# One block's gate projection as three float32r passes, and two sets of weight splits placed elsewhere

## The chip, the cores and the metric

The kernel runs on one core of one Trainium2 chip. The core has TensorE (PE: matmuls; PEld is its weight load), VectorE (DVE), ScalarE (ACT), GpSimd (POOL), SyncE (SP, which here issues the transfers) and DMA engines. The metric is the device time of the whole program in microseconds (us), less being better.

## The reference

The input x has 4 sequences of 1024 tokens with 512 features. Two sublayers follow one another, each as x + LN(f(LN(x))), where LN subtracts the mean and divides by the standard deviation.

- Retention: q = x Wq', v = x Wv', g = silu(x Wg'), all 512 wide. A scan over the tokens keeps state = lam * state + v for each feature, with lam set by `beta`; y = q * state is normalised over the features, scaled by gamma, shifted by beta, multiplied by g and projected by Wo.
- FFN: gate = silu((x Wgate) * scale), up = (x Wup) * scale, both 1536 wide; the product is projected back to 512 by Wdown. These three weights are rounded to 8-bit floats first.

## The kernel before

**Blocks.** The 4096 tokens are worked on as 8 blocks of 512 tokens (`NB` = 8, `TB` = 512), features on the partitions in 4 chunks of 128. A `Retention` object works one block through the first sublayer, an `Ffn` object one block through the second in 12 steps i = 0 to 11 (`gate`, `up`, `fuse`, `rest`, `down`). While the FFN of block t runs, the retention of block t+1 is woven into its steps. Blocks 0 and 1 come ahead of that loop: a straight list of calls (the "opening" in what follows) normalises and projects block 0 (object `a`) and projects block 1 (object `b`), and prepares weights.

**Order.** Every compute engine's instructions are kept in the order in which the Python code issues them (`InOrder`, which is line 75 in the profile, so that nearly every row there reads L75). An instruction that has to wait holds up all that follows on its engine. Waits come from data and from buffers.

**Two kinds of matmul.** In float32 one matmul instruction of 128x512 does it. In float32r the operands have fewer bits, so an exact product takes three passes over split operands: `top` (the upper bits), `low` (the rest, scaled), `diff`. `begin(k, c, home)` runs the passes top and low of column c of projection k into a PSUM bank and then has ACT multiply the bank by 1 + 2^-12 (the "rescale"); `end(k, c)` runs the pass diff on top of that and then uses the bank: for v two half scans and a copy of the carry on DVE, for q a product on DVE and a sum on POOL, for g a silu on ACT. Block 0 uses float32 for v, q, g and o (`v`, `q`, `gate`, `o`); block 1 uses passes for v, q and g, with weights in SBUF; blocks 2 to 7 use passes throughout, with weights that a ring of transfers brings (`w_ring`).

**Banks.** PSUM banks are named by `home`: `pa0` and `pa1`, two banks that share the name `pf` and are given out in turn, and `pd0` to `pd3`. In the opening the `pf` banks go to v and g of block 0, then to block 1; later the FFN's `gate` and `up` use them.

**Splits.** `Splitter.split(n)` prepares one 128-column unit of a weight: DVE cuts the upper bits, subtracts, and forms `diff`; ACT then scales `low`. Units 0 to 3 are of v, 4 to 7 of q, 8 to 11 of g, 12 to 15 of o. `store(n)` sends the parts to DRAM for the later blocks. In SBUF they lie in five slots taken in turn. The table `times` places the splits of o into block 1's FFN steps (keys are the FFN's block, step and place in it).

**FFN weights.** `rounds(n)` advances a generator that rounds FFN weights piece by piece: one DVE cast to 8 bits, one ACT copy into `gate_sb`, `up_sb` or `down_sb`, and an empty turn, with the load of a next piece in between.

**Block 0's norm of y.** `mean` averages y over the features by a matmul (`mu`), `center_y` subtracts it on DVE, squares on ACT and sums on POOL (`sqsum`; the squares have two buffers); `var`, `rstd_y` and `z` finish it, and `o` projects.

## Time and profile before

| | |
|---|---|
| median of 3 runs | 897.91 us (895.42 to 899.96) |
| the profiled execution | 896.99 us, of which 895.2 us is the span from first to last instruction |
| mean granted TensorE clock | 0.997 of full |
| PE busy | 879.5 us, 98% of the span |
| DVE busy | 627.0 us, 70% |
| ACT busy | 419.0 us, 47% |
| POOL busy | 234.1 us, 26% |

"Busy" is the time in which an engine has an instruction under way; idle time of an engine that is not the bottleneck costs nothing. Durations of matmuls overlap one another, so the spacing of their starts, not the duration of one, is what a stream of them costs.

### The profile page before, as it was taken

Reading aid. Unit: us, or ns where it says so; the run is one execution under the profiler, and the core shown is the slowest. Engines: PE = TensorE matmul, PEld = TensorE weight load, DVE = VectorE, ACT = ScalarE, POOL = GpSimd, SP = SyncE. Lnnn points to the kernel's source line nnn. Section 1 sums busy time; section 2 is a strip of 40 time slices with the busy share of each in tenths; the row PEclk is TensorE's granted clock in tenths of the full one; section 3 lists DMA queues with packets and bytes.
Section 4 is the critical chain, followed back from the end, with each engine's and each line's share of the span. In section 5 each row is a group of like instructions: output and inputs, shape, how many; then the busy total and the mean of one; then the engine's idle time right before and its main releaser. Section 6 shows DMA issues by size and latency. Waiting matters only on the chain.

```text
span 895.2 us, 11996 instructions
## 1 busy us (share of the span) xinstructions
PE 879.5 (98%) x3948; PEld 739.1 (83%) x3948; DVE 627.0 (70%) x1074; ACT 419.0 (47%) x741; POOL 234.1 (26%) x301
## 2 busy tenths in 40 slices
PE   9999999999999999999999999999999999999996
PEld 7466786788888888888888888888888888888885
DVE  4898796686777666876678675876758756665635
ACT  1369566433645336453454435453364533644323
POOL 1215203302414033230513214150232403322020
PEclk9999999999999999999999999999999999999998
DMA  8975544687464674556662765627745464424021
GB/s 283 288 240 180 179 148 147 170 249 251 131 169 149 204 235 146 137 172 214 220 173 71 250 205 178 188 72 247 236 140 153 143 210 141 140 96 118 1 95 50
DMA packets 115576, 152.67 MB, mean 171 GB/s; under 512 B 10867, under 2 KB 54644, under 8 KB 115444
## 3 DMA queue, kind: packets, MB, share of 16 engines
q1 hardware_dynamic: 114644, 151.18, 55.4%
q8 instruction: 33, 0.54, 0.2%
q10 hardware_dynamic: 864, 0.66, 0.2%
q14 instruction: 35, 0.29, 0.1%
HBM read 117.46 MB, written 38.54 MB: 174 GB/s over the span
## 4 chain that ended last, share of the span: by engine, by line
PE 84%; DVE 2%; ACT 1%; issue 0%; DVEq 0%
PE pfu L75 18%; PE pfg L75 18%; PE pd L75 17%; PE po L75 8%; PE pv L75 7%; PE pq L75 7%; PE pg L75 7%; PE mu L75 1%; PE pt L75 1%; PE var L75 0%; DVE gate L75 0%; DVE y L75 0%; DVE d L75 0%; DVE split_room L75 0%; DVE x1nT L75 0%
## 5 line engine op out<-in xcount | busy, mean ns | idle before, releaser
L75 PE MATMUL pfu<-x1nT,up_sb 128*128 128x512 f32 x768 | 183.1, 381 | 0.0
L75 PE MATMUL pfg<-x1nT,gate_sb 128*128 128x512 f32 x768 | 182.5, 380 | 0.1
L75 PE MATMUL pd<-down_sb,fuse 128*128 128x512 f32 x720 | 170.5, 379 | 0.0
L75 PEld LDWEIGHTS pfu<-x1nT,up_sb 128*128 128x128 f32 x768 | 145.1, 189 | 22.5 <-issue 1.7
L75 PEld LDWEIGHTS pfg<-x1nT,gate_sb 128*128 128x128 f32 x768 | 144.4, 189 | 22.6 <-ACT gate L75 1.9
L75 PEld LDWEIGHTS pd<-down_sb,fuse 128*128 128x128 f32 x720 | 141.4, 196 | 14.5
L75 DVE SCALAR_TENSOR_TENSOR gate<-pfu,us_sb,gate 128x512 f32<-128x512 f32 x96 | 71.7, 747 | 68.9 <-PE pfu L75 57.8
L75 ACT CAST fuse<-gate 128x512 fp32r<-128x512 f32 x90 | 55.6, 618 | 126.4 <-DVE gate L75 125.4
L75 ACT ACTIVATE gate<-pfg,gs_sb 128x512 f32<-128x512 f32 x96 | 65.7, 684 | 98.0 <-PE pfg L75 98.0
L75 POOL TENSOR_SCALAR mv<-mv 128x1 f32<-128x1 f32 (+1 forms) x82 | 22.1, 270 | 322.7 <-DVE mv L75 320.6
L75 DVE TENSOR_TENSOR fuse<-gate,fuse 128x512 fp32r<-128x512 f32 x90 | 69.9, 777 | 6.6 <-ACT fuse L75 6.4
L75 POOL TENSOR_TENSOR d<-d,x 128x512 f32<-128x512 f32 x28 | 42.1, 1524 | 84.5 <-ACT d L75 70.6
L75 DVE BATCH_NORM_STATS2 st<-x 128x6 f32<-128x512 f32 x64 | 43.5, 680 | 17.9 <-POOL x L75 15.1
L75 POOL TENSOR_TENSOR mv<-mv,nhalf 128x1 f32<-128x1 f32 (+1 forms) x75 | 52.1, 694 | 6.2
L75 POOL TENSOR_TENSOR x<-x,x1n 128x512 f32<-128x512 f32 x32 | 44.4, 1394 | 21.6 <-ACT x1n L75 17.4
L75 ACT ACTIVATE pv<-pv 128x512 f32<-128x512 f32 x28 | 16.3, 582 | 47.8 <-PE pv L75 47.8
L75 POOL TENSOR_TENSOR ysum<-y 128x512 f32<-128x512 f32 x8 | 10.6, 1324 | 106.7 <-DVE y L75 106.7
L75 DVE TENSOR_TENSOR y<-pq,y 128x512 f32<-128x512 f32 x28 | 19.1, 681 | 21.5 <-PE pq L75 21.5
L75 DVE BATCH_NORM_STATS2 st<-po 128x6 f32<-128x512 f32 x32 | 21.9, 684 | 14.3 <-PE po L75 14.3
L75 ACT ACT_TABLE_LOAD x19 | 24.4, 1283 | 15.0 <-DVE var L75 10.8
L75 POOL TENSOR_TENSOR sqsum<-sqsum,sq 128x512 f32<-128x512 f32 x21 | 29.2, 1389 | 7.2 <-PE pg L75 5.5
L75 DVE SCALAR_TENSOR_TENSOR y<-y,lnb_sb,mids 128x512 f32<-128x512 f32 x28 | 26.0, 928 | 7.1 <-ACT mids L75 7.0
(216 smaller groups left out, 1482.5 us busy)
## 6 DMA issues: line engine op xcount, KB each, us to landing
x<-in_x SPq DMA_DIRECT2D x52, 256.0 KB, 5.3
kept<-x SPq DMA_DIRECT2D x32, 256.0 KB, 3.2
x<-kept SPq DMA_DIRECT2D x32, 256.0 KB, 4.2
out<-d SPq DMA_DIRECT2D x31, 256.0 KB, 2.0
w_ring<-dtop_v SPq DMA_DIRECT2D x24, 256.0 KB, 4.3
w_ring<-dlow_v SPq DMA_DIRECT2D x24, 256.0 KB, 3.1
w_ring<-ddiff_v SPq DMA_DIRECT2D x24, 256.0 KB, 3.9
w_ring<-dtop_q SPq DMA_DIRECT2D x24, 256.0 KB, 2.6
```

The source lines that it names most:

```text
L75: return lambda *args, **kwargs: tc.keep_in_program_order(op(*args, **kwargs))
```

## The change

- **Block 0's g** is no longer four float32 projections but `begin` and `end` as in block 1. New code, `new_parts` and `parts_of_x`, makes the parts of block 0's normalised x early in the opening: for each quarter three DVE instructions and one ACT copy, into the parts of `gate_sb`, `up_sb` and `down_sb` that hold no FFN weights yet. The order becomes begin 0; mean and centring; begin 1, end 0; begin 2, end 1; begin 3, end 2, end 3. `gate`, `silu` and `g_of` go.
- **`end` is cut in two**, `close` (the diff pass) and `finish` (what uses the bank), and in block 1's v and q the DVE work is placed anew: `split(5)`, `split(6)` and `split(7)` come ahead of scans that they followed, and one FFN weight cast comes earlier.
- **`split` of o is cut in two**, DVE's three instructions and ACT's scaling (`lower`, letter l in `times`). In step 5 of block 1's FFN the DVE parts of units 14 and 15 both come at its start, ahead of `fuse`; the ACT parts come later.

The core of the diff:

```diff
-            act.activation(low, m, AF.Copy, scale=1.0 / LOW)
             self.at_work[n] = {"diff": diff} if k == "o" else {"diff": diff, "low": low}
+            self.lows[n] = low
+            if k != "o":
+                self.lower(n)
+        def lower(self, n):
+            low = self.lows.pop(n)
+            act.activation(low, low.bitcast(F32), AF.Copy, scale=1.0 / LOW)
...
-            (0, 11, "mid"): "w12 w13 w14 w15", (1, 0, "start"): "r s12", (1, 0, "mid"): "s13",
-            (1, 0, "end"): "k12", (1, 1, "start"): "k13", (1, 5, "start"): "s14",
-            (1, 5, "mid"): "k14 s15", (1, 5, "end"): "k15",
+            (0, 11, "mid"): "w12 w13 w14 w15", (1, 0, "start"): "r s12", (1, 0, "mid"): "l12 s13",
+            (1, 0, "end"): "k12", (1, 1, "start"): "l13 k13", (1, 5, "start"): "s14 s15",
+            (1, 5, "mid"): "l14 k14", (1, 5, "end"): "l15 k15",
...
+        def new_parts(self):
+            self.tops, self.low = (w[:, :, 2 * P : 2 * P + TB] for w in (gate_sb, up_sb))
+            self.diff = down_sb[:, 2 : 2 + NC, :]
+        def parts_of_x(self, k):
+            top = work.tile([P, D], F32, tag="tok", name=f"top_{self.t}_{k}", bufs=4)
+            top = top.rearrange("p (c g j) -> p c g j", c=NC, j=Q)
+            x, low, diff = self.quarter(self.xnT, k), self.quarter(self.low, k), self.quarter(self.diff, k)
+            dve.tensor_scalar(top.bitcast(I32), x.bitcast(I32), TOP_MASK, None, ALU.bitwise_and)
+            act.copy(self.quarter(self.tops, k), top)
+            dve.tensor_tensor(low, x, top, ALU.subtract)
+            dve.scalar_tensor_tensor(diff, low.bitcast(F32), -1.0 / LOW, top, ALU.mult, ALU.add)
...
+    a.new_parts()
+    for k in range(2):
+        a.parts_of_x(k)
     decay()
+    for k in range(2, NS):
+        a.parts_of_x(k)
...
-    a.g_of(0, "pf")
+    a.begin("g", 0, "pf")
     a.mean()
     a.center_y()
     splitter.store(11)
-    a.g_of(1, "pf")
+    a.begin("g", 1, "pf")
+    a.end("g", 0)
     b.cut_x(2)
     b.cut_x(3)
     rounds(3)
-    a.g_of(2, "pf")
+    a.begin("g", 2, "pf")
+    a.end("g", 1)
     splitter.split(0)
-    a.gate(3, "pf")
-    a.silu(3)
+    a.begin("g", 3, "pf")
+    a.end("g", 2)
+    a.end("g", 3)
     a.var()
...
     a.o_moments(3)
+    rounds(1)
     a.x1_moments(2)
     a.x1_of(3)
-    b.end("v", 0)
+    b.close("v", 0)
     b.begin("v", 2, "pd0")
+    b.finish("v", 0)
     a.x1n_of(2)
     a.rest_of(0)
-    b.end("v", 1)
+    b.close("v", 1)
     a.turn_x1n(1)
     a.upper_of(1)
+    b.begin("v", 3, "pd1")
+    splitter.split(5)
+    splitter.store(4)
     a.x1_moments(3)
-    b.begin("v", 3, "pd1")
     a.x1n_of(3)
     a.rest_of(1)
-    splitter.split(5)
-    splitter.store(4)
-    b.end("v", 2)
+    b.close("v", 2)
     a.turn_x1n(2)
     a.upper_of(2)
     b.begin("q", 0, "pd2")
-    a.rest_of(2)
-    b.end("v", 3)
-    b.begin("q", 1, "pd3")
     splitter.split(6)
     splitter.store(5)
+    b.finish("v", 1)
+    a.rest_of(2)
+    b.close("v", 3)
+    b.begin("q", 1, "pd3")
     a.turn_x1n(3)
     a.upper_of(3)
-    b.end("q", 0)
+    b.close("q", 0)
     splitter.split(7)
     splitter.store(6)
+    b.finish("v", 2)
+    b.finish("q", 0)
+    b.begin("q", 2, "pf")
+    b.close("q", 1)
     a.rest_of(3)
-    b.begin("q", 2, "pf")
-    b.end("q", 1)
-    rounds(1)
+    b.finish("v", 3)
+    b.finish("q", 1)
     b.begin("q", 3, "pf")
     b.end("q", 2)
-    rounds(2)
     b.end("q", 3)
     splitter.store(7)
-    rounds(3)
+    rounds(5)
```

More of the change, by code (lines that the diff above doesn't have):

```diff
@@ L330, in __init__ @@
             self.raw = {}
-            self.slots, self.slot_of, self.at_work = [], {}, {}
+            self.slots, self.slot_of, self.at_work, self.lows = [], {}, {}, {}
         def by_chunk(self, ap):
@@ L403, in sandwich @@
             (0, 1, "end"): "c12", (0, 2, "end"): "c13", (0, 3, "end"): "c14", (0, 4, "end"): "c15",
[3 rows of a table removed]
[3 rows of a table added]
         }
         def at(self, *when):
-            do = {"c": self.copy, "s": self.split, "k": self.store, "w": self.keep}
+            do = {"c": self.copy, "s": self.split, "l": self.lower, "k": self.store, "w": self.keep}
             for what in self.times.get(when, "").split():
@@ L607, in pass_of @@
                 w = splitter.part(k, c, part)
-            x = {"top": self.by_chunk, "low": self.low, "diff": self.diff}[part]
+            x = {"top": self.by_chunk if self.passes else self.tops, "low": self.low, "diff": self.diff}[part]
             for i in range(NC):
@@ L626, in end, with close, finish @@
         def end(self, k, c):
-            bank = self.bank.pop((k, c))
-            self.pass_of(bank, k, c, "diff")
-            bank = in_order(bank)
+            self.close(k, c)
+            self.finish(k, c)
+        def close(self, k, c):
+            self.pass_of(self.bank[k, c], k, c, "diff")
+        def finish(self, k, c):
+            bank = in_order(self.bank.pop((k, c)))
             if k == "v":
@@ L651, in end @@
                     pool.tensor_tensor(self.sum, self.sum, y[:, c, :], ALU.add)
-            else:
-                act.activation(self.new_mids()[:, c], bank, AF.Silu)
+            elif self.passes:
+                act.activation(self.new_mids()[:, c], bank, AF.Silu)
+            else:
+                home = big if c == 3 else work
+                tag, bufs = ("fuse", 3) if home is big else ("sg", 3)
+                self.g[c] = home.tile([P, TB], F32, tag=tag, name=f"g_{self.t}_{c}", bufs=bufs)
+                act.activation(self.g[c].rearrange("p (k u) -> p k u", k=2), bank, AF.Silu)
         def gap(self, n):
@@ L814, in rstd_y @@
             )
-        def gate(self, c, home="pa"):
-            self.pg[c] = ps_tile(f"pg_{self.t}_{c}", home)
-            project(self.pg[c], wg_sb, c, [self.by_chunk])
-        def silu(self, c):
-            home = big if c == 3 else work
-            tag, bufs = ("fuse", 3) if home is big else ("sg", 3)
-            self.g[c] = home.tile([P, TB], F32, tag=tag, name=f"g_{self.t}_{c}", bufs=bufs)
-            act.activation(self.g[c], self.pg.pop(c), AF.Silu)
-        def g_of(self, c, home="pa"):
-            self.gate(c, home)
-            self.silu(c)
         def scale_y(self, c):
```

## The prediction

> **What bounds the kernel now.** I read the page's busy shares and its chain first, then TensorE's waits, then the timelines around the three edits.

> ```profile
> PE 879.5 (98%) x3948; PEld 739.1 (83%) x3948; DVE 627.0 (70%) x1074; ACT 419.0 (47%) x741; POOL 234.1 (26%) x301
> PE 84%; DVE 2%; ACT 1%; issue 0%; DVEq 0%
> ```

> TensorE is the bound; only fewer PE cycles or fewer PE waits can save time. The waits view of PE lists all it ever waited for; its two largest entries are the targets of the second and third edit.

> ```profile
> PE pg L75 <- ACT pg L75: 2.4, 1, 2.4
> PE pq L75 <- ACT slot L75: 2.1, 1, 2.1
> ```

> The timeline of PE where the first edit falls (start, length of the group, count):

> ```profile
> 36.72 3.60 PE L75 MATMUL pq<-xnT,wq_sb 128*128 128x512 f32 x8
> 40.16 3.60 PE L75 MATMUL pg<-xnT,wg_units 128*128 128x512 f32 x8
> 43.59 1.02 PE L75 MATMUL mu<-ysum,mean_r 128*128 128x512 f32 x2
> 44.45 10.46 PE L75 MATMUL pg<-xnT,wg_units 128*128 128x512 f32 x24
> 54.75 1.02 PE L75 MATMUL var<-sqsum,mean_r 128*128 128x512 f32 x2
> ```

> No bracket with an idle time stands here: PE runs through. ACT in the same stretch:

> ```profile
> 43.81 0.63 ACT L75 ACTIVATE gate_sb<-gate_sb 128x512 fp32r<-128x512 f32 x1 [4.06 <-DVE gate_sb L75]
> 44.41 0.62 ACT L75 CAST down_sb<-top 128x512 fp32r<-128x512 f32 x1
> 45.05 1.28 ACT L75 ACT_TABLE_LOAD   x1
> 46.34 0.60 ACT L75 ACTIVATE g<-pg 128x512 f32<-128x512 f32 x1
> 46.84 0.62 ACT L75 ACTIVATE sqsum<-y 128x512 f32<-128x512 f32 x1
> 47.35 1.14 ACT L75 ACTIVATE sq<-y 128x512 f32<-128x512 f32 x2
> 49.36 0.63 ACT L75 ACTIVATE sq<-y 128x512 f32<-128x512 f32 x1 [0.87 <-POOL sqsum L75]
> ```

> The last square waits for POOL's first sum. The silu of g 0 stands ahead of the squares here; after the change it stands behind them.

> **Part 1, block 0's g.** Removed: four columns of 3.43 us (40.16 to 43.59), 13.7. Added: 48 float32r matmuls; the chain's rows have 8 in 1.73 us, 0.216 each, so 10.4. On PE alone that saves 3.4 us.

> The new parts of x: per quarter the split rows' spacing, 0.45 + 0.72 + 0.65 = 1.8 us of DVE, 7.3 for four, and four ACT copies of 0.6. ACT idles from 13.6 to 28.7. DVE has pauses of 3.25, 2.31, 0.32, 1.21 and 1.13 us between 10.35 and 24.87, 8.2 together. Walked in order, with `lam` behind two of the ACT copies, the first scan starts at about 18.7 instead of 16.28, and DVE has caught up when the second product of y is due at 24.87. Nothing on PE needs those scans before v 2 takes their bank at 24.67. I cost it at nothing; without that cover it would be up to 2 us, of which block 1's first transpose (31.5, its input ready at 30.1) still hides 1.4.

> Now the stretch from 40.16. PE does top and low of g 0 until 41.9, waits for POOL's sum of y (41.19 + 1.31) and does the mean from 42.55 to 43.4, then top and low of g 1 until 45.1. ACT rescales g 0 behind the cast that ends at 45.0, so at 45.5, and PE runs diff of g 0 until 46.4. Next on PE is g 2, and the two `pf` banks hold g 0 and g 1: it needs the silu of g 0. In ACT's new order that comes behind all squares, the rescale of g 1 and the table load. DVE's centring still starts at 45.02 (its queue before it, product, split 11 and cut, is unchanged); the squares run from 45.75, the second ends at 46.95, POOL's sum takes 1.31 from 47.05, the last square runs from 48.4 to 49.0, rescale of g 1 to 49.55, load 1.28 to 50.85, silu 0.6 to 51.45. PE stands from 46.4 to 51.5: 5.1 us, and everything on PE is queued behind. Then g 2 until 53.2, diff of g 1 until 54.1; ACT's silu of g 1 ends at 54.9 and frees the bank for g 3, 54.95 to 56.7; diff of g 2 until 57.55, of g 3 until 58.4. `var` starts at 58.4 instead of 54.75: **3.65 us later**, not 3.4 earlier. Without the second wait it would be 2.8. From `var` on, DVE's norm of y and PE's order follow as before (block 1's g, then o, with no PE pause from 55.2 to 97 in the old trace), so the shift goes through.

> A pause of 5.1 us also touches the clock. The windows view at the end of the span, where PE's last matmul ends at about 887.4 (columns: stretch, busy times and counts by engine, granted clock, DMA share, GB/s):

> ```profile
> 888.00:890.00 2.00, 0.00 (x0) 0.00 (x0) 1.93 (x6) 0.73 (x2) 0.00 (x0) 0.85 0.36 131
> 890.00:892.00 2.00, 0.00 (x0) 0.00 (x0) 1.01 (x4) 0.00 (x0) 0.00 (x0) 0.50 0.56 202
> ```

> A mean of 0.85 is 1.4 us at full and 0.6 at half: the clock fell at 889.4, some 2 us after the last matmul. The pauses of 2.07 and 2.36 us inside the span left it at 1.00. How long a return takes shows at the start: of the 40 records of warm-up matmuls 16 are over by 5.0 us (4 a us from 1.0), the next 12 by 6.5 (8 a us): some 4 us at half pace. So the pause costs between 0 and 4 / 2 = 2.0 us more. I take 1.5, near the rows that show a fall and a slow return; less than the full 2.0 since a fall late in the pause leaves less to pay.

> [...]

> **Part 2, the last q splits.** PE waits 2.07 us until 99.23 for the low part of unit 6, whose DVE split starts at 96.65 behind two scans. Moved ahead of the scan of v 1, it ends near 93.2 in old times, its scaling at 93.8; q 2's low is due at 97.0. That wait goes. What is late next: q 2's product on DVE, which frees the bank of the FFN's first gate matmul. DVE works without a pause from 84.90 to 102.02, and all of it but nothing more stays ahead of that product; the cast now goes into the 1.80 us pause before 84.90 instead. So the product ends at 102.7 at the earliest and the FFN starts at 102.75, not 104.67: **1.9 us** saved; 2.07 is the most, and 0.9 remains if one moved instruction takes the 1.65 us of the slow split rows near 41 and 244 instead of 0.69. SP passes one load ahead of a store of x, two issues of some 0.4 us with nobody waiting; POOL's order is unchanged.

> **Part 3, o's splits of step 5.** PE waits 2.36 us until 248.28 for the rescale of g 3, queued on ACT behind unit 15's scaling, which waits for DVE. In the new order DVE does both splits from 237.81 (1.82 each), so `fuse` 5 starts at 241.45, not 239.99; behind it wait ACT's cast, a silu, two norms and POOL's adds. The rescale of g 3 comes at 245.3 and PE goes on at 245.9. But gate 7 needs the bank that the silu of gate 6 frees, and on ACT that silu stands behind three casts of y, which wait for DVE. Block 2 does this step without splits; DVE, ACT and PE there:

> ```profile
> 348.99 0.75 DVE L75 SCALAR_TENSOR_TENSOR gate<-pfu,us_sb,gate 128x512 f32<-128x512 f32 x1 [2.10 <-PE pfu L75]
> 349.65 2.73 DVE L75 SCALAR_TENSOR_TENSOR y<-y,gamma_sb,rstd 128x512 f32<-128x512 f32 x4
> 352.30 1.76 DVE L75 SCALAR_TENSOR_TENSOR y<-y,lnb_sb,mids 128x512 f32<-128x512 f32 x1
> 354.10 1.38 DVE L75 TENSOR_SCALAR y_cut<-y 128x512 int32<-128x512 int32 x1
> ```
> ```profile
> 358.35 0.68 ACT L75 ACTIVATE gate<-pfg,gs_sb 128x512 f32<-128x512 f32 x1
> ```
> ```profile
> 359.08 1.99 PE L75 MATMUL pfg<-x1nT,gate_sb 128*128 128x512 f32 x8
> ```

> Beside POOL's adds (351.66 to 355.2) the first product and cut are slow, 1.76 and 1.38 where their neighbours take 0.74 and 0.43. From `fuse` 5 to the silu's end are 359.03 - 348.99 = 10.04 us. With `fuse` 5 at 241.45, and unit 15's scaling (0.55) now ahead of that silu, it ends at 252.05 and gate 7 starts at 252.1, where the old trace has 252.71: **0.6 us** saved. If POOL's adds slow nothing, all 2.4; I take the row of block 2.

> **Sum.** The profiled execution took 896.99 us (span 895.2, 1.8 around it). + 3.65 + 1.5 - 1.9 - 0.6 = + 2.65, so 899.6. The median of the runs is 0.9 above that execution: 900.6.

> **The rivals.**
> - *The clock holds* at full through the pause, as it did through 2.36 us. Then + 1.15: 899.1 on the median, or 897.3 with part 3's full 2.4.
> - *The pause does not come*, because ACT reaches the silu of g 0 in time. Then PE's own price counts: - 3.4 - 1.9 - 2.4 = - 7.7, 890.2. Against it: the order on ACT and the two banks are fixed in the program, and the old trace's centring, POOL sum and table load have durations that leave no room.
> - *Slower*: the half clock outlasts the restart. From the restart to `var` PE has 28 matmuls of 0.216, 6.05 us; all at half pace they cost 6.05 more instead of 1.5: + 7.2, 905.1. It decides from a clock loss of 3.35 us on. For it: after the pause PE waits once more for a bank (0.85 us). Against it: 4 us sufficed at the start.

> That float32r passes are not cheaper can't be: block 1's own g runs 8 of them in 1.73 us.

> **How the numbers follow.** Forecast (pause with some clock loss) 0.45; clock holds 0.22; no pause 0.10; long half clock 0.18; 0.05 for a new wait in the moved scans. About 0.5%, 4.5 us, is what a measurement of this kernel can tell from no change. Faster by more than that takes the second rival: 0.10. Slower: the third, the new wait and the forecast's upper edge, 0.27. Within: 0.63. The forecast's own bounds are 898.0 (2.8 for the pause, no clock loss, part 2 at 2.07) to 902.1 (clock 2.0, part 2 at 0.9); runs scatter by 2.3 around the median. 895 to 905 leaves out the second rival and the upper half of the third.

> **What would show it.** Right: a PE wait of about 5 us for ACT's g near 46.4 to 51.5, a granted clock under 1.00 just after, `var` near 58.4; no wait for slots near 97; a wait of nearly 2 us before gate 7 of block 1 in place of 2.4 before g 3. Wrong: PE without a pause between 40 and 55, or a first scan that pushes block 1's transposes past 31.5.

## The result, and the profile after

| | before | after |
|---|---|---|
| median | 899.2 us (895.42 to 901.27, 6 runs) | 903.56 us (902.52 to 904.52, 6 runs) |
| profiled execution | 896.99 us, span 895.2 | 902.52 us, span 900.7 |
| mean granted TensorE clock in it | 0.997 | 0.994 |

The change makes the kernel slower by half a percent: ratio 1.0052, 95% interval 1.0033 to 1.0072. The forecast was 900.6 with a range of 895 to 905. One execution of those below, of `e2_splits_only`, took 1154.58 us at a mean granted clock of 0.752; the figures leave it out.

The page of the kernel after (busy time; then the chain that ended last, by engine):

```profile
PE 879.5 (98%) x3964; PEld 743.3 (83%) x3964; DVE 632.7 (70%) x1086; ACT 423.2 (47%) x749; POOL 233.5 (26%) x301
PE 80%; issue 2%; DMA 1%; DVE 1%; POOL 1%; ACT 1%; SPq 0%; POOLq 0%; ACTq 0%; DVEq 0%
```

PE is busy for the same 879.5 us as before, though its work became less: part of it ran at half clock, where, as shown below, four matmuls count as busy for 2.08 us instead of 1.13. Its largest waits (us in total, times, longest):

```profile
PE pg L75 <- ACT g L75: 5.4, 2, 4.7
PE pfg L75 <- ACT gate L75: 1.9, 2, 1.7
PE pq L75 <- ACT pq L75: 1.8, 2, 1.4
...
PE pfg L75 <- DVE y L75: 0.7, 1, 0.7
```

The two old entries, 2.4 for g's rescale and 2.1 for the slots, are gone; 5.4 us for the silu of g, 1.9 for a gate's silu and 0.7 for a product of q on DVE are new. The entry for the rescale of q stood at 0.5 before; it differs as much between executions without the change and returns below. PE's timeline where the old one ran through (the first row is the last product of q, from whose start `var` is measured below):

```profile
35.75 3.60 PE L75 MATMUL pq<-xnT,wq_sb 128*128 128x512 f32 x8
...
44.61 1.13 PE L75 MATMUL pg<-down_sb,slot 128*128 128x512 f32 x4 [0.17 <-ACT pg L75]
50.45 2.08 PE L75 MATMUL pg<-gate_sb,wg_units 128*128 128x512 f32 x4 [4.71 <-ACT g L75]
...
56.62 1.13 PE L75 MATMUL pg<-gate_sb,wg_units 128*128 128x512 f32 x4 [0.69 <-ACT g L75]
...
60.32 1.02 PE L75 MATMUL var<-sqsum,mean_r 128*128 128x512 f32 x2
```

And ACT's, in the order that the prediction gave for it:

```profile
47.37 0.63 ACT L75 ACTIVATE sq<-y 128x512 f32<-128x512 f32 x1 [0.78 <-POOL sqsum L75]
47.91 0.58 ACT L75 ACTIVATE pg<-pg 128x512 f32<-128x512 f32 x1
48.51 1.28 ACT L75 ACT_TABLE_LOAD   x1
49.80 0.60 ACT L75 ACTIVATE g<-pg 128x512 f32<-128x512 f32 x1
```

Four matmuls took 2.08 us at 50.45 where the same four take 1.13 at 56.62. The windows view shows why (stretch, PE's busy time and count, granted clock, DMA share, GB/s):

```profile
48.00:50.00 2.00, 0.00 (x0) 0.87 1.01 315
50.00:52.00 2.00, 1.55 (x4) 0.50 0.96 278
...
54.00:56.00 2.00, 1.94 (x5) 0.50 1.00 313
56.00:58.00 2.00, 1.38 (x6) 0.92 1.12 357
```

The trace's clock record has the exact times: half speed from 49.49 to 56.32 us, so for 6.83 us. Last, block 1's step 5 on DVE, ACT and PE:

```profile
250.05 1.76 DVE L75 SCALAR_TENSOR_TENSOR y<-y,lnb_sb,mids 128x512 f32<-128x512 f32 x1
251.85 1.39 DVE L75 TENSOR_SCALAR y_cut<-y 128x512 int32<-128x512 int32 x1
```
```profile
256.64 0.67 ACT L75 ACTIVATE gate<-pfg,gs_sb 128x512 f32<-128x512 f32 x1
```
```profile
257.36 1.99 PE L75 MATMUL pfg<-x1nT,gate_sb 128*128 128x512 f32 x8 [1.68 <-ACT gate L75]
```

The same slow pair on DVE as in block 2, and the wait before gate 7 behind it, as forecast.

### The profile page after: what moved, and what is told of

Its sections match the earlier page's. It is cut to its first block, busy times and chain, and to the rows that moved or that the text cites. A ratio compares the mean times of both kernels' runs of the same rounds, so it can differ in the third digit from the quotient of the medians.

```text
span 900.7 us, 12051 instructions
## 1 busy us (share of the span) xinstructions
PE 879.5 (98%) x3964; PEld 743.3 (83%) x3964; DVE 632.7 (70%) x1086; ACT 423.2 (47%) x749; POOL 233.5 (26%) x301
## 4 chain that ended last, share of the span: by engine, by line
PE 80%; issue 2%; DMA 1%; DVE 1%; POOL 1%; ACT 1%; SPq 0%; POOLq 0%; ACTq 0%; DVEq 0%
PE pfg L75 17%; PE pfu L75 17%; PE pd L75 17%; PE po L75 8%; PE pv L75 7%; PE pq L75 6%; PE pg L75 6%; DMA mx<-xs 1%; PE mu L75 1%; PE pt L75 1%; POOL d L75 0%; PE var L75 0%; POOL sqsum L75 0%; DVE gate L75 0%; DMA w_ring<-ddiff_o 0%
## 5 line engine op out<-in xcount | busy, mean ns | idle before, releaser
L75 PE MATMUL pfg<-x1nT,gate_sb 128*128 128x512 f32 x768 | 182.4, 380 | 2.6 <-ACT gate L75 1.9
L75 PE MATMUL pfu<-x1nT,up_sb 128*128 128x512 f32 x768 | 183.1, 381 | 0.0
L75 PE MATMUL pd<-down_sb,fuse 128*128 128x512 f32 x720 | 170.5, 379 | 0.0
L75 PEld LDWEIGHTS pfg<-x1nT,gate_sb 128*128 128x128 f32 x768 | 144.5, 189 | 25.1 <-ACT gate L75 3.6
L75 PEld LDWEIGHTS pfu<-x1nT,up_sb 128*128 128x128 f32 x768 | 145.1, 189 | 22.5 <-issue 1.7
L75 PEld LDWEIGHTS pd<-down_sb,fuse 128*128 128x128 f32 x720 | 141.4, 196 | 14.5
L75 DVE SCALAR_TENSOR_TENSOR gate<-pfu,us_sb,gate 128x512 f32<-128x512 f32 x96 | 71.8, 747 | 68.5 <-PE pfu L75 58.3
L75 ACT CAST fuse<-gate 128x512 fp32r<-128x512 f32 x90 | 55.6, 618 | 134.6 <-DVE gate L75 133.7
L75 ACT ACTIVATE gate<-pfg,gs_sb 128x512 f32<-128x512 f32 x96 | 65.6, 684 | 98.2 <-PE pfg L75 98.2
L75 POOL TENSOR_SCALAR mv<-mv 128x1 f32<-128x1 f32 (+1 forms) x82 | 21.9, 267 | 328.7 <-DVE mv L75 326.6
L75 DVE TENSOR_TENSOR fuse<-gate,fuse 128x512 fp32r<-128x512 f32 x90 | 70.0, 777 | 7.0 <-ACT fuse L75 6.5
L75 POOL TENSOR_TENSOR d<-d,x 128x512 f32<-128x512 f32 x28 | 41.8, 1512 | 85.9 <-ACT d L75 72.0
L75 DVE BATCH_NORM_STATS2 st<-x 128x6 f32<-128x512 f32 x64 | 43.5, 680 | 17.2 <-POOL x L75 14.5
L75 POOL TENSOR_TENSOR mv<-mv,nhalf 128x1 f32<-128x1 f32 (+1 forms) x75 | 52.9, 705 | 6.2
L75 POOL TENSOR_TENSOR x<-x,x1n 128x512 f32<-128x512 f32 x32 | 44.4, 1394 | 21.7 <-ACT x1n L75 17.5
L75 ACT ACTIVATE pv<-pv 128x512 f32<-128x512 f32 x28 | 16.3, 582 | 48.7 <-PE pv L75 48.7
L75 POOL TENSOR_TENSOR ysum<-y 128x512 f32<-128x512 f32 x8 | 10.2, 1276 | 107.2 <-DVE y L75 107.2
L75 DVE TENSOR_TENSOR y<-pq,y 128x512 f32<-128x512 f32 x28 | 18.9, 681 | 20.0 <-PE pq L75 20.0
L75 DVE SCALAR_TENSOR_TENSOR y<-y,lnb_sb,mids 128x512 f32<-128x512 f32 x28 | 27.0, 965 | 7.6 <-ACT mids L75 7.5
L75 DVE BATCH_NORM_STATS2 st<-po 128x6 f32<-128x512 f32 x32 | 21.9, 685 | 14.3 <-PE po L75 14.3
L75 POOL TENSOR_TENSOR sqsum<-sqsum,sq 128x512 f32<-128x512 f32 x21 | 28.8, 1371 | 6.2 <-ACT sq L75 4.5
```

What stands on the lines that cost most here:

```text
L75: return lambda *args, **kwargs: tc.keep_in_program_order(op(*args, **kwargs))
```

## The experiments

Each group of runs had its own runs of the kernel before beside it, on the same chip; their medians were 898.9 to 899.7. Ratios are to those. Times "after q 3" are from the start of block 0's last product of q to the start of `var`; in before they are 54.75 - 36.72 = 18.03 us.

| run | median us | ratio to before (95%) | mean clock |
|---|---|---|---|
| e1_g_only | 907.18 | 1.0097 (1.0064 to 1.013) | 0.992 to 0.994 |
| e2_splits_only | 894.86 | 0.9951 (0.9935 to 0.9967) | 0.997 to 0.998 |
| e3_warm | 902.51 | 1.0049 (1.0033 to 1.0065) | 0.997 to 0.998 |
| e4_silu_first | 903.1 | 1.0044 (1.0027 to 1.0061) | 0.993 to 0.997 |
| e5_banks | 895.22 | 0.9955 (0.994 to 0.997) | 0.997 to 0.999 |
| e6_late_adds | 901.06 | 1.0021 (1.0007 to 1.0035) | 0.993 to 0.996 |
| e7_fill | 898.98 | 0.9993 (0.9981 to 1.0005) | 0.997 to 0.998 |
| e8_cleared | 894.9 | 0.9952 (0.9939 to 0.9966) | 0.997 to 0.998 |
| e9_cleared_old_g | 893.72 | 0.9942 (0.992 to 0.9965) | 0.997 to 0.999 |
| e10_last_d | 890.65 | 0.9912 (0.9892 to 0.9932) | 0.997 to 0.998 |
| e11_before_last_d | 896.55 | 0.9968 (0.9957 to 0.998) | 0.993 to 0.998 |
| e12_fill_last_d | 895.14 | 0.9951 (0.9934 to 0.9969) | 0.997 to 0.998 |

### The parts apart

`e1_g_only` is the changed kernel with block 1's splits, scans and weight casts, and o's splits, in the old order; `e2_splits_only` is the reverse. From the changed kernel to e1, and to e2:

```diff
-    b.close("v", 0)
+    b.end("v", 0)
     b.begin("v", 2, "pd0")
-    b.finish("v", 0)
...
-            (1, 0, "end"): "k12", (1, 1, "start"): "l13 k13", (1, 5, "start"): "s14 s15",
-            (1, 5, "mid"): "l14 k14", (1, 5, "end"): "l15 k15",
+            (1, 0, "end"): "k12", (1, 1, "start"): "k13", (1, 5, "start"): "s14 l14",
+            (1, 5, "mid"): "k14 s15 l15", (1, 5, "end"): "k15",
```
```diff
-    a.begin("g", 0, "pf")
+    a.g_of(0, "pf")
...
-    a.begin("g", 1, "pf")
-    a.end("g", 0)
+    a.g_of(1, "pf")
...
```

> Block 0's g by passes alone; q's and o's splits as before. Theory (the pause for the silu of g 0 costs 6.5 us from the last q product to var, 3.65 of it standing and 2.9 of it half clock; the two split edits give back about 1.5 and 0.7): 6.5 us above before, var some 24.6 us after the start of q 3 instead of 18.0, and the old waits of 2.1 us for slots near 103 and 2.4 us before g 3's diff are back. Rival A (the new waits later on, at mu, at a q diff near 219 and before gate 7, are what costs): without the split edits the kernel is within 3 us of before. Rival B (the early parts of x on DVE delay block 1): a wait of PE for transposes or v near 24 to 35.

> Block 0's g in float32 as before; q's and o's splits as in the change. Theory: 1.9 to 2.3 us below before (q 1.2 to 1.6, o 0.7); the FFN's first gate matmul waits 0.7 us for DVE's q product, gate 7 waits 1.7 us for ACT's silu; g runs through without a pause at full clock. Rival A (the moved scans and splits cost more later than they save): at or above the time of before, with a wait for a q rescale near 214.

Measured: + 8.3 and - 4.0 us against 898.88, together + 4.3, as much as the change's 4.4. So the parts add, part 1 alone loses, and the splits gain. But both are larger than expected, by 1.7 us and more. In e2's nine runs the mean clock never came below 0.997; the runs of the kernel before stand from 0.993 to 0.998, and their times go with it (correlation -0.88 over 24 runs): five at 0.998 average 897.0 us, ten at 0.996 average 898.7, six at 0.993 and 0.994 about 901. The profiled execution of before belongs with the first five: it has no fall inside its span. In e1's trace one of the old pauses is caught at it. PE's timeline and, after it, PE's windows:

```profile
104.46 1.13 PE L75 MATMUL pq<-gate_sb,slot 128*128 128x512 f32 x4 [2.08 <-ACT slot L75]
```
```profile
104.00:106.00 2.00, 1.54 (x6) 0.92 0.69 261
106.00:108.00 2.00, 2.00 (x6) 0.50 0.01 1
```

The clock fell at 105.67, 1.2 us after PE had resumed from a pause of 2.08 us, and stayed at half until 109.08. The same pause, 2.07 us, stands in the kernel before. With this fall the stretch from `var` to the FFN's first gate took 51.61 us, and 49.92 in before: 1.69 us for one fall.

### The clock, and what makes the pause

`e3_warm` keeps PE busy through the pause with 22 unused 128x128 matmuls; `e4_silu_first` puts diff and silu of g 0 ahead of ACT's squares.

```diff
     a.end("g", 0)
+    idle = ps_d.tile([P, P], F32, tag="pd0", name="idle_g")
+    warm(22)
```
```diff
     a.mean()
+    a.begin("g", 1, "pf")
+    a.end("g", 0)
     a.center_y()
     splitter.store(11)
-    a.begin("g", 1, "pf")
-    a.end("g", 0)
```

> The change with 22 unused 128x128 float32 matmuls put on PE behind the diff pass of g 0, where it would stand for 4.7 us; they are done before the silu of g 0. Theory (clock): PE still gets to g 2 only when that silu is done, but at full clock; var comes 2.6 to 2.9 us earlier relative to q 3 (about 21.8 us after it instead of 24.6), total 2.6 us below the change. Rival B (the half clock is hidden behind the second wait for ACT): less than 1 us below the change.

> The change with begin of g 1 and end of g 0 issued ahead of centring, so that the table load and the silu of g 0 come ahead of the squares on ACT. Theory (the order on ACT makes the pause): the pause before g 2 falls from 4.7 to about 1.6 us (rescale to 45.0, load 1.3, silu 0.6), the clock stays full, g 3 waits for ACT behind the squares for some 2 us at most, and var comes 18 to 19.5 us after q 3 instead of 24.6: 5 to 6 us below the change, so 1 to 2 us below before. Rival A (the two banks make it, whatever the order on ACT): the pauses add up to 4 us or more again and the time stays within 2 us of the change.

PE's timeline of e3:

```profile
36.57 3.60 PE L75 MATMUL pq<-xnT,wq_sb 128*128 128x512 f32 x8
...
58.52 1.02 PE L75 MATMUL var<-sqsum,mean_r 128*128 128x512 f32 x2
```

e3: no fall of the clock inside the span, and var starts 21.95 us after q 3's start (before 18.03, after 24.57). So the pauses, with what the passes themselves save or add, cost 3.92 us, the clock 2.62 more in the profiled execution. The total, though, was only 1 us below the change, where 2.6 was expected; why is not known. e4: the waits are 2.03 us before g 2 and 3.27 before g 3, 5.30 together against 5.40. The rival held: with two banks, one wait or the other was there in both of the orders tried on ACT.

### g on four banks

```diff
-    a.begin("g", 1, "pf")
-    a.end("g", 0)
...
+    a.begin("g", 2, "pd0")
+    a.close("g", 0)
...
+    a.begin("g", 3, "pd1")
+    a.close("g", 1)
+    a.close("g", 2)
+    a.close("g", 3)
+    for c in range(NC):
+        a.finish("g", c)
```

> The changed kernel, but g 2 and g 3 of block 0 take the banks pd0 and pd1, which block 1's cuts have left, instead of the two pf banks, and the four silus come together behind all passes. Theory (the pause is made by the two pf banks, and the half clock by the pause): PE waits for no silu of g any more, the granted clock stays at 1.00 there, and var comes about 15.5 us after q 3's start (before 18.03, change 24.57). With the two saved pauses of parts 2 and 3, worth 3.9 us in the run without part 1, the total is 2.5 below that run's 895.0: about 892.4. Rival 1 (float32r passes for g cost PE as much as they save): var at 18 or later and 895 or more. Rival 2 (what follows var is not ready: the norm of y and block 1's parts on DVE and ACT were hidden by the old, later var): var at 15.5, but a new PE wait behind it and 894 to 896.

No wait for a silu of g is left, the clock holds, and var comes 15.80 us after q 3: the passes do save PE 2.2 us there. So the two banks made the pause: without it the total is some 8 us below the change. But it equals that of the splits alone within their intervals; rival 2 held. PE's timeline behind the stage:

```profile
101.57 1.99 PE L75 MATMUL pfg<-x1nT,gate_sb 128*128 128x512 f32 x8 [1.54 <-DVE y L75]
...
109.43 0.49 PE L75 MATMUL mu<-half,mean_r 128*128 128x512 f32 x1 [0.68 <-ACT half L75]
```

In e2 these two waits were 0.70 and 0.33. What g saves is waited for again at DVE's product of q 2 and at the halves of y's sum: from q 3 to the FFN's third gate e5 is ahead of e2 by 1.05 us, not 2.2.

### POOL's adds

```diff
-                for s in (2, 3):
+                for s in (2, 3) if t > 1 else ():
...
                 b.split_y(*range(NC))
+                for s in (2, 3) if t == 1 else ():
+                    l.norm_shifted(s)
+                    l.add(s)
```

> The changed kernel, but in block 1 the norms and POOL's adds of the last two x rows come one step later (behind the split of y). Theory (POOL's adds stretch DVE's first product and cut of y from 0.74 to 1.76 and from 0.43 to 1.39 us, and so hold the casts and the silu before gate 7): the two rows come down to 0.74 and 0.43, PE's wait of 1.7 us before gate 7 goes, and the total is 1 to 1.7 us below the change's 903.3, less what the adds cost where they now fall. Rival (the wait is the order on ACT alone, whatever DVE's speed): wait 1.7 us as before, total 903 to 904.

The theory held. DVE's timeline of e6:

```profile
248.69 0.74 DVE L75 SCALAR_TENSOR_TENSOR y<-y,lnb_sb,mids 128x512 f32<-128x512 f32 x1
249.47 0.43 DVE L75 TENSOR_SCALAR y_cut<-y 128x512 int32<-128x512 int32 x1
```

With POOL's adds at 257.81 instead of 249.41 the pair is as fast as its neighbours, the wait of 1.68 us before gate 7 is gone, and one of 0.40 is new at o. The slowness went along with the adds: DVE's product `fuse` beside them, at 259.77, took 1.75 us where the next one took 0.68. The edit moves two norms on ACT as well, but in the changed kernel ACT stood idle for 2.23 us behind them, until the slow cut came, so they did not hold the silu. The median went down by 2.5 us; the ratios, 1.0052 and 1.0021, say about 2.8, more than the wait itself; their intervals overlap slightly, so that the size is uncertain.

### The old pauses filled, and the DMA behind q

`e7_fill` is the kernel before, with unused matmuls in its two pauses:

```diff
             self.pass_of(bank, k, c, "top")
+            if (self.t, k, c) == (1, "q", 2):
+                fill(ps_d, "pd0", 8)
...
                 if what == "end":
+                    if (self.t, k, c) == (2, "g", 3):
+                        fill(ps_a, "pa0", 9)
```

> The kernel before, with 8 and 9 unused 128x128 matmuls in its two pauses of 2.07 and 2.36 us (ahead of the low pass of q 2 and of the last pass of g 3); nothing else is changed. Theory (these pauses trip the clock in most executions, 1.7 us each time): the pauses are all but gone as idle time, the mean granted clock is 0.998 in all runs, and the median falls from 898.9 to about 897, with little scatter. Rival (the scatter and the splits' extra gain have another cause, and a pause of 2 us never touches the clock): 898 to 900 with the scatter of the kernel before.

Half of it came. The clock was 0.997 to 0.998 in all ten runs and the scatter shrank to 1.5 us. But the median, 898.98, lay only 0.7 below the kernel before, which the interval does not tell from nothing. The profile of e7 suggests what stood in the way: waits of PE for the rescale of q, 2.7 us in all where the profiled execution of before had 0.5. They hang on DVE's last product of d in each middle block, which waits until a DMA has read the buffer that it writes. In e8, the worst of them; DVE, then PE:

```profile
423.33 0.69 DVE L75 TENSOR_TENSOR d<-pd,ds_sb 128x512 f32<-128x512 f32 x1 [1.71 <-DMA mx<-xs]
```
```profile
427.27 1.13 PE L75 MATMUL pq<-diff,w_ring 128*128 128x512 f32 x4 [1.41 <-ACT pq L75]
```

In the eleven profiles of kernels that keep this order (before, after, e1 to e9) the entry for q was between 0.5 and 3.7 us. So I tried the later waits, and this one by itself:

`e8_cleared` is e5 with its waits behind g taken away, `e9_cleared_old_g` the same with float32 g, `e10_last_d` is e8 with the late product of d. The edits that e8 has beside e5's and e6's, then the one that e10 adds:

```diff
-    b.begin("q", 2, "pf")
+    b.begin("q", 2, "pa0")
...
-    b.begin("q", 3, "pf")
+    b.begin("q", 3, "pd0")
...
+            if t == 0 and i == 0:
+                b.halves(False)
             f.fuse(i)
+            if t == 0 and i == 0:
+                b.lower_half()
...
```
```diff
-                for s in range(NS if b else NS // 2):
+                for s in range(NS - 1 if b else NS // 2):
                     l.scale(s)
...
             f.fuse(i)
+            if l and b and i == 2:
+                l.scale(NS - 1)
```

> The kernel of e5 (g by passes on four banks, splits as changed) with the three waits that its profile shows behind that stage taken away: the last two q of block 1 take the banks pa0 and pd0, so that the first gate of the FFN need not wait for q 2's product (1.54 us); ACT's and DVE's halves of the sum of y come one gate earlier (waits of 0.68 and 0.23 us for block 1's mean); and block 1's late adds come as in e6 (1.68 us before gate 7). Theory (what g's passes save was lost again at these waits): 1.54 + 0.9 + 1.7 - 0.4 = 3.7 us less than e5's 895.2, about 891.5, a ratio of 0.991 to the kernel before. Rival (DVE's queue bounds that step, and the waits come back at var, at o or at a later gate): 893 to 895.

> The same three waits taken away, but block 0's g as in the kernel before (plain matmuls, two pf banks). The difference to e8 is what the float32r passes of g are worth where nothing behind them waits. Theory: 2.2 us, the difference of var's start after q 3 (15.8 in e5, 18.03 before), so about 893.7. Rival (the passes are worth no more than between e5 and the splits alone, which differ by 0.5 us of span): within 0.6 us of e8.

> e8, and in each middle block DVE's last product of d, which waits 0.3 to 1.3 us for the DMA that reads the buffer it writes, comes behind the product of q 1 and the gate's product instead of ahead of them. Theory (that DMA wait makes the waits of PE for the rescale of q, 0.5 to 3.6 us in all by execution, and with them most of the scatter that the clock leaves): these waits all but vanish, the total falls 0.5 to 2 us below e8, and the runs scatter less. Rival: the norm of d becomes late instead, and the total stays within 0.5 us of e8 or rises.

In e8 the three waits are gone (new are 0.37 us at q 3, 0.28 at a gate and 0.41 at o), yet its total is no better than e5's: its profile has 3.7 us of waits for q, e9's has 0.7. From q 3 to the third gate, ahead of those, e8 leads e9 by 1.40 us, which is what the passes of g are worth there; in the medians e9 is 1.2 us ahead. That the waits for q make this difference is argued from one profile of each and not shown. Without these waits e10 takes 890.65 us, 4.2 below e8, twice the most that was expected, and beats both kernels: 0.9912 of before. Its profile has the shortest span of all, 887.8 us, with PE busy for 99% of it:

```profile
PE 875.7 (99%) x3964; PEld 741.3 (83%) x3964; DVE 632.1 (71%) x1086; ACT 422.3 (48%) x749; POOL 233.2 (26%) x301
```

The last pair puts the same edit into the kernel before (e11) and into e7 (e12), to see the clock's price without the DMA's scatter.

> The kernel before with one edit, the one that e10 adds to e8: in each middle block DVE's last product of d comes behind the product of q 1 and the gate's product. Theory (the scatter of the kernel before has two sources, falls of the clock at its two pauses, 1.7 us each, and PE's waits for the rescale of q, which hang on a DMA): the waits for q are gone, the two pauses of 2.07 and 2.36 us stay, and the times go with the clock alone: some 895.5 to 896.5 at 0.998, 1.7 more at 0.996, 3.4 more at 0.994; median 0.5 to 2 us below the kernel before. Rival (e10's gain over e8 was not the DMA wait but its run): within 0.5 us of the kernel before.

> The kernel before with both that edit and the unused matmuls of e7 in its two pauses. Theory (with the DMA wait out of the way, e7's clock effect shows in the time): clock 0.997 to 0.998 in all runs, and a median 1.5 to 2 us below the run without the unused matmuls (about one fall of 1.7 us in the mean execution). Rival (falls of the clock are not what the pauses cost beyond their idle time): within 0.5 us of it.

Both theories held in kind, with other sizes. The waits for q are gone from both profiles. e11 is 3.2 us below the kernel before, more than the 2 expected, and still has two runs of 895.1 and 895.2 at 0.998, seven of 896.2 to 897.0 at 0.995 and 0.996, and two of 898.0 and 899.1 at 0.993 (one run fits badly: 898.4 at 0.997). e12 lies at 894.8 to 895.7 in all five, 1.4 below e11's median, where 1.5 to 2 were expected. e11's own trace shows the second old pause with a fall; PE's timeline and windows:

```profile
247.49 1.50 PE L75 MATMUL pg<-diff,w_ring 128*128 128x512 f32 x4 [2.36 <-ACT pg L75]
```
```profile
248.00:250.00 2.00, 2.00 (x6) 0.53 0.68 159
```

## Why the prediction was right, and where it was not

- **Part 1 without the clock: right.** ACT's order, the silu of g 0 at 51.45 and `var` 3.65 us later were forecast; with after's opening 0.97 us earlier (q 3's start lies between 35.35 and 36.72 us in the profiles, with no order by kernel), the silu ended at 51.37 on the old scale, the second wait was 0.69 instead of 0.85, and e3 gives 3.92. The early parts of x cost nothing, as argued: DVE's second product of y, at 23.90, still stands behind 0.59 us of idle time.
- **The clock: the step that failed** was "The pauses of 2.07 and 2.36 us inside the span left it at 1.00". That held for the one execution in the profile. Over many, the same pauses bring the mean clock of the kernel before down to 0.9957 (0.998 without falls): some 2 us, an estimate from this share; where unused matmuls kept the clock up, 1.4 us were gained (e12 against e11). So the clock was no cost of the new pause alone, but a cost that was there and that parts 2 and 3 took away. In the profiled execution of after the new pause cost 2.6 instead of 1.5 us, above the upper bound of 2.0. The pause reached 0.96 us into the first 3.41 us at half clock, and a second stretch of 3.41 us followed; in e1, where the same pause of 4.72 us ended together with the fall at 51.06, one was all, and `var` came 23.62 us after q 3, 1.67 later than in e3. In the medians the forecast's 1.5 is nearly met, by luck: the clocks of after's six runs average 0.9945, 0.0012 below before's 24, which is 1.1 us over the span, but this is a new loss less an old one that went.
- **Part 2: 1.56 us instead of 1.9**, measured from `var` to the FFN's first gate, with the forecast reason: PE now waits 0.70 us there for DVE's product of q 2. The 0.34 us between are the first row of the moved split 5, 0.77 us where the old one had 0.42.
- **Block 1's mean: 0.35 us that the forecast did not have.** PE waits there for ACT's and DVE's halves of the sum of y. It goes with part 1: from the FFN's first gate to its third, after takes 8.93 us and e1 8.92, before 8.56 and e2 8.57. What in part 1 makes it stays open.
- **Part 3: 0.71 us instead of 0.6**, with the wait before gate 7 where it was put; e6 shows that POOL's adds make it.
- **The base**: "The median of the runs is 0.9 above that execution" took the scatter for noise around it. It was a low one, with no fall of the clock and with 0.5 us of waits for q; over six runs the median is 2.2 above it.
- **The sum.** 3.92 - 1.56 + 0.35 - 0.71 = 2.0 without the clock, 3.1 with 1.1 for it; measured were 4.4. The ratio's interval is 3.0 to 6.5 us, so 3.1 is still inside it; the remaining 1.3 us are not settled. They are within what the waits for q vary by, and the same holds for e1's 2 us above its terms and for e3, which should have been 2.6 and was 1 us below the change.

Of the rivals, "the clock holds" and "the pause does not come" did not occur, and "the half clock outlasts the restart" in part: half clock lasted 5.9 us from the restart at 50.45 on, longer than the 4 us taken from the start of the span, but cost 2.6 us and not the 3.35 from which it would have decided. e1, e3 and e4 show the pause, filled or in two pieces in the last two, as long as g has two banks, and e5, with four, has none.

## What to carry to other kernels

One profiled execution of a kernel can miss a cost that most of its executions pay: where the times of the runs go with the mean clock, look for pauses of PE that only sometimes trip it, and ask of an edit whether it adds or takes away such a pause. A wait taken off the bound engine is worth only the distance to the next late thing, so walk on to that one (here three more waits, each cheap to move, though their gain did not show in the total while the waits for q stood) before counting the gain. And a queued instruction that waited for a DMA held all behind it (1.71 us on DVE in e8, and behind them 1.41 on PE): putting two that don't need it ahead was worth 3.2 us here in one kernel and 4.2 in another, about as much as parts 2 and 3 together (4.0).
